# A two-layer decoder on one core: three experts of the third batch moved to the end, a two-expert distance in the last batch, and the last pair's row sums on two engines

## The chip, the core and the metric

The kernel runs on one core of one Trainium2 chip. A core has a matrix engine (TensorE, PE in the profile, with its weight loads as PEld), a vector engine (VectorE, DVE), an activation engine (ScalarE, ACT), a general engine (GpSimd, POOL) and SyncE (SP), which here only issues DMA transfers. Each engine runs its own instructions in order and waits for others by semaphores. The metric is the device time of one execution in microseconds, the median of several.

## The reference

There are four batches of 256 tokens, each token a row of 256 numbers. A batch passes through six residual steps; each normalises its input and adds its result to `x`. The last two matter here:

```python
x = x + _L1_xattn_ref(_layernorm(x), ctx_2048, ...)      # 16 query heads, 4 key heads, 1857 keys
x = x + _L1_ffn_ref(_layernorm(x), w_gate, wi_0, wi_1, wo)

# inside _L1_ffn_ref, 8 experts, 2 chosen per token
logits = jnp.dot(xf, w_gate)
top_logits, top_idx = jax.lax.top_k(logits, K)
weights = jax.nn.softmax(top_logits, axis=-1)
...
h0 = jax.lax.ragged_dot(sorted_x, wi_0, group_sizes)
h1 = jax.lax.ragged_dot(sorted_x, wi_1, group_sizes)
inter = jax.nn.silu(h0) * h1
out_sorted = jax.lax.ragged_dot(inter, wo, group_sizes)
```

The attention step is a softmax over 1857 keys for each of 16 heads; the heads are grouped by four on one key head. All of it is float32.

## The kernel before

**The step loop.** The cross attention of all four batches is one loop of steps (`steps`, L1329). A `Pair` (L1160) is two query heads of one batch and key head: 32 pairs in all, and each has eight chunks of keys (`NPAIR`), seven of 256 keys and a last one of 65. For each chunk, `score` (L1169) makes the scores `bsc` (two key blocks of 128 keys by 512 columns), copies them to `s` on ACT and keeps a running maximum `acc` on DVE. When a pair's scores are complete, `maximum` (L1188) transposes `acc` (`tm`), reduces it, and spreads it over the partitions (`bc`). Ten steps behind the scores, `exponential` (L1201) subtracts `bc` on DVE, takes the exponential on ACT and adds the chunk into `sum` on GpSimd: one addition for the first chunk (L1209), then one per key block (L1212). One step later, `weigh` (L1214) multiplies the chunk with the values into `bpo`. `finish` (L1223) copies `bpo` to `aT` on ACT, adds `sum` over the partitions with eight small matmuls (`ts`, L1232), takes the reciprocal `rs`, multiplies by the output weights (`bpw`, L1241), and adds into `x` on DVE (L1245). It is a generator in four pieces.

**Side work in the loop.** Other work is cut into generator pieces, and `put` (L1263) gives each piece a numbered place, two per step; `others` runs the pieces of a place. This is how the next key head is prepared and how the experts of batches 0, 1 and 2 are run (L1316 to L1320), 23 pieces each. The experts of batch 3 can't start before the last pair has been added into `x`, so they run alone at the very end (L1397).

**The experts.** `experts(b)` (L849) has seven pieces for normalisation, transposes (`tp`), features `yTm`, gate scores `pl`, the choice of two experts and their weights `gts`. After that there are two pieces per expert: one makes `mph` (four products, which the profile counts as eight matmuls), its `it` by a tanh on ACT and two operations on DVE (L919 to L921); the other makes `mpe` (two products, four matmuls) and adds it, weighted, into `x` with two DVE operations (L927). All eight experts are computed for every token, with weight zero for those not chosen. Weights `wi` (two transfers) and `we` (one) are loaded by SP for two experts at a time, into the `db` buffers (three of them, L162) and the `a3` buffers (three, L154). `it`, the normalised rows `mxh` and `yTm` share three buffers of the tag `a2`. PSUM products take turns over six banks (`p1`, L131).

**What sets the order.** The order of instructions on each engine is fixed when the program is built. The builder follows the written order, but if an instruction isn't ready by the builder's own estimate of times, a later one on that engine that is ready goes ahead of it. On the chip, each engine then keeps this order.

Of the kernel before, what the change touches and what calls it, by code (L numbers as in the profile page):

```python
# [15 lines left out]
AF = mybir.ActivationFunctionType  # L16
# [17 lines left out]
NROPE = 3  # L34
TERN = 20
SIDE = 24
SIDEN = 4
RATE = 1
START = (0, 3, 9, 15)
# [70 lines left out]
def decoder_kernel(ctx: ExitStack, tc: tile.TileContext, at, t, out):  # L110
# [43 lines left out]
    def fa(b, name, dt=F32):  # L154

        return fr.tile([P, 512], dt, tag=f"a{b}", name=name, bufs=NA)
# [686 lines left out]
        yield  # L843


    def ea(name):
        return fa(2, name)

    def experts(b):  # L849
        xb = xs[b]  # L850
        wgt = sm([P, 2, NE], "wgt", f"wgt{b}", 1)
        nc.sync.dma_start(out=wgt, in_=t["wgt"].rearrange("(c p) n -> p c n", p=P))
        s8 = [P, 2, NE]
        iota = cc("iota8")[:, None, :].to_broadcast(s8)
        mv = moments(xb, f"mo{b}")
        yield
        r1 = rsqrt(mv[:, :, 1], 1e-5, f"mo{b}")
        yield
        xh = centred(ea(f"mxh{b}"), xb, mv, r1)
        yield  # L860
        tp = to_features(xh, f"mo{b}")
        yT = ea(f"yTm{b}")
        A.copy(yT, tp)
        yT = yT.rearrange("p (c t) -> p c t", c=2)
        yield
        pl = p1(f"pl{b}")
        for j in range(2):
            for c in range(2):
                T.matmul(pl[:, j * 8 : j * 8 + 8], lhsT=yT[:, c, j * P : (j + 1) * P], rhs=wgt[:, c, :], start=c == 0, stop=c == 1)
        lg = sm(s8, "lg", f"mlg{b}", 1)  # L870
        V.tensor_copy(lg.rearrange("p j e -> p (j e)"), pl[:, 0:16])
        yield

        tops, hots = [], []
        for k in range(2):
            m = sm([P, 2], f"m{k}", f"mm{b}{k}", 1)
            V.tensor_reduce(m, lg, AX.X, ALU.max)
            oh = sm(s8, f"oh{k}", f"oh{b}{k}", 1)
            V.tensor_tensor(oh, lg, m[:, :, None].to_broadcast(s8), ALU.is_equal)
            V.tensor_mul(oh, oh, iota)  # L880
            ix = sm([P, 2], "ix", f"ix{b}{k}", 1)
            V.tensor_reduce(ix, oh, AX.X, ALU.min)
            V.tensor_tensor(oh, iota, ix[:, :, None].to_broadcast(s8), ALU.is_equal)
            if k == 0:
                V.scalar_tensor_tensor(lg, oh, NEG, lg, ALU.mult, ALU.add)
            tops.append(m)
            hots.append(oh)
        w2 = sm([P, 2], "w2", f"w2{b}", 1)
        V.tensor_sub(w2, tops[1], tops[0])
        A.activation(w2, w2, AF.Exp)  # L890
        yield
        w1 = sm([P, 2], "w1", f"w1{b}", 1)
        V.tensor_scalar(w1, w2, 1.0, None, ALU.add)
        V.reciprocal(w1, w1)
        V.tensor_scalar(w1, w1, 0.5, None, ALU.mult)
        V.tensor_mul(w2, w2, w1)
        gts = sm(s8, "gts", f"gts{b}", 1)
        V.tensor_mul(gts, hots[0], w1[:, :, None].to_broadcast(s8))
        V.tensor_mul(hots[1], hots[1], w2[:, :, None].to_broadcast(s8))
        V.tensor_add(gts, gts, hots[1])  # L900
        yield
        for e2 in range(0, NE, 2):
            wi = db(f"wi{b}{e2}").rearrange("p (i c n) -> p i c n", i=2, c=2)
            for i, name in enumerate(("wi0", "wi1")):
                nc.sync.dma_start(
                    out=wi[:, i], in_=t[name][:, e2 * ME : (e2 + 2) * ME].rearrange("(c p) n -> p c n", p=P)
                )
            we = weight(fa(3, f"we{b}{e2}"), "woe", e2 * ME, (e2 + 2) * ME, 0, D)
            for f in range(2):
                e = e2 + f  # L910
                ph = p1(f"mph{b}{e}")
                for i in range(2):
                    for c in range(2):
                        T.matmul(  # L914
                            ph[:, i * 256 : i * 256 + 256], lhsT=wi[:, i, c, f * ME : (f + 1) * ME], rhs=yT[:, c, :],
                            start=c == 0, stop=c == 1,
                        )
                it = ea(f"it{b}{e}")[:, 0:256]
                A.activation(it, ph[:, 0:256], AF.Tanh, scale=0.5)  # L919
                V.scalar_tensor_tensor(it, it, 1.0, ph[:, 0:256], ALU.add, ALU.mult)  # L920
                V.tensor_mul(it, it, ph[:, 256:512])  # L921
                yield
                pe = p1(f"mpe{b}{e}")
                for j in range(2):
                    T.matmul(pe[:, j * 256 : j * 256 + 256], lhsT=it[:, j * P : (j + 1) * P], rhs=we[:, f, :], start=True, stop=True)  # L925
                for j in range(2):
                    V.scalar_tensor_tensor(  # L927
                        xb[:, j, :], pe[:, j * 256 : j * 256 + 256], gts[:, j, e : e + 1], xb[:, j, :], ALU.mult, ALU.add
                    )
                yield  # L930
        nc.sync.dma_start(out=out[b].rearrange("(j p) d -> p j d", p=P), in_=xb)
        yield

    def before(b):
# [225 lines left out]
    class Pair:  # L1160


        def __init__(self, b, g, h):
# [2 lines left out]
            self.rows = [P] * (NPAIR - 1) + [LAST]  # L1166
            self.wide = [2] * (NPAIR - 1) + [1]

        def score(self, c):  # L1169

            e = gt[self.b, self.g]
            q = e["qT"][:, self.h : self.h + 2, :].rearrange("p h t -> p (h t)")
            n, w = self.rows[c], self.wide[c]
            s = s_tile(f"s{self.nm}{c}")
            self.s.append(s)
            if c == 0:
                self.acc = fa(0, f"acc{self.nm}")
            for i in range(w):
                k = 2 * c + i
                pc = p1(f"bsc{self.nm}{k}")  # L1180
                T.matmul(pc[0:n, :], lhsT=e["kT"][:, k * P : k * P + n], rhs=q, start=True, stop=True)  # L1181
                A.activation(s[0:n, i, :], pc[0:n, :], AF.Copy, scale=e["kn"][0:n, k : k + 1])  # L1182
                if k == 0:
                    V.tensor_scalar(self.acc, pc, e["kn"][:, 0:1], None, ALU.mult)  # L1184
                else:
                    V.scalar_tensor_tensor(self.acc[0:n, :], pc[0:n, :], e["kn"][0:n, k : k + 1], self.acc[0:n, :], ALU.mult, ALU.max)  # L1186
# [14 lines left out]
        def exponential(self, c):  # L1201
            n, w, s = self.rows[c], self.wide[c], self.s[c]
            V.tensor_tensor(  # L1203
                s[0:n, 0:w, :], s[0:n, 0:w, :], self.bc[0:n, None, :].to_broadcast([n, w, 512]), ALU.subtract
            )
            A.activation(s[0:n, 0:w, :], s[0:n, 0:w, :], AF.Exp)  # L1206
            if c == 0:
                self.sum = fr.tile([P, 512], F32, tag="sum", name=f"sum{self.nm}", bufs=2)
                G.tensor_tensor(self.sum, s[:, 0, :], s[:, 1, :], ALU.add)  # L1209
            else:  # L1210
                for i in range(w):
                    G.tensor_tensor(self.sum[0:n, :], self.sum[0:n, :], s[0:n, i, :], ALU.add)  # L1212
# [10 lines left out]
        def finish(self):  # L1223
# [4 lines left out]
            yield  # L1228

            ts = p1(f"ts{nm}")  # L1230
            for i in range(4):
                T.matmul(ts[:, i : i + 1], lhsT=su[:, i * P : (i + 1) * P], rhs=cc("ones")[:, 0:1], start=True, stop=True)  # L1232
            rs = sm([P, 4], "rs", f"rs{nm}")
            V.reciprocal(rs, ts[:, 0:4])
            yield

            for h in range(2):
                pw = p1(f"bpw{nm}{h}")
                for j in range(2):
                    o = h * 256 + j * P  # L1240
                    T.matmul(  # L1241
                        pw[:, j * 256 : j * 256 + 256], lhsT=aT[:, o : o + P], rhs=e["wo"][:, self.h + h, :], start=True, stop=True
                    )
                for j in range(2):
                    V.scalar_tensor_tensor(  # L1245
                        xs[b][:, j, :], pw[:, j * 256 : j * 256 + 256], rs[:, 2 * h + j : 2 * h + j + 1], xs[b][:, j, :], ALU.mult, ALU.add
                    )
                yield


    heads = [(b, g) for b in range(B) for g in range(NKV)]
# [31 lines left out]
    for n, pair in enumerate(pairs):  # L1283
# [4 lines left out]
        e += DW  # L1288
        gen = pair.finish()
        put(2 * e + 1, gen)  # L1290
        put(2 * e + 4, gen, bank=True)
        put(2 * e + 7, gen, bank=True)
        put(2 * e + 10, gen, True, bank=True)
    for k, (b, g) in enumerate(heads):
        base = 32 * (k - 1)
        if k:
# [19 lines left out]
    for b in range(B - 1):  # L1316
        gen = experts(b)
        spot = 2 * (64 * (b + 1) + 17)
        for i in range(23):
            spot = put(spot, gen, i == 22, i not in (0, 1, 2, 5, 6)) + (5 if i > 6 else 3)  # L1320

    def others(place):
        for gen, last in places.pop(place, ()):
# [70 lines left out]
    run(first)  # L1394
    run(work)
    assert not places, sorted(places)
    run(experts(B - 1))  # L1397


# [63 lines left out]
```

## Time and profile before

| | us |
|---|---|
| median of 3 runs (1830.79 to 1831.85) | 1831.21 |
| the profiled execution | 1831.5 |
| its span, first to last instruction | 1829.5 |
| TensorE busy | 1727.7 (94%) |
| DVE busy | 1300.5 (71%) |
| ACT busy | 1008.2 (55%) |
| POOL busy | 872.4 (48%) |
| mean granted TensorE clock | 0.968 |

A busy share is the time in which an engine had an instruction running, over the whole span. TensorE's share is high, but it is a mean over stages that have different limits. The page's slices of the span say more: TensorE is at nine tenths or more from the tenth slice to the 39th, and at seven in the last. The chain that ended last, followed back from the last instruction, is 70% TensorE, 10% DVE, 8% ACT, 7% POOL and 4% "issue", time in which an engine waited for nothing that the profile shows. Timeline rows give start, length, engine, line, operation, the tiles written and read, and in brackets the idle time before it and who ended that.

### The profile page before, as it was taken

How to read it: one execution, taken by the hardware profiler on the slowest of the kernel's cores; microseconds unless marked ns; L12 is line 12 of the kernel's file. 1: busy time of each engine (PE TensorE's matmuls, PEld its weight loads, DVE VectorE, ACT ScalarE, POOL GpSimd, SP SyncE). 2: the span in 40 equal slices, each digit the busy share in tenths (PEclk: the TensorE clock that was granted, in tenths of full speed). 3: DMA queues.
4: the chain of work that ended last, by engine and by line, in shares of the span. 5: the costliest groups of instructions: out<-in, count | busy, mean ns of one | idle time of the engine just before them, and what ended most of it. 6: DMA issues, size and time to landing. Idle time of an engine off the chain costs nothing.

```text
span 1829.5 us, 20298 instructions
## 1 busy us (share of the span) xinstructions
PE 1727.7 (94%) x6576; PEld 1054.0 (58%) x6576; DVE 1300.5 (71%) x2444; ACT 1008.2 (55%) x1896; POOL 872.4 (48%) x716
## 2 busy tenths in 40 slices
PE   3779899989999999999999999999999999999997
PEld 2456686655555555555555555656565655556555
DVE  6785647786777678777767786767768676766764
ACT  1556636463666565665656565565656465555541
POOL 2100232111266566656657475555656565655470
PEclk8689999989999999999999999999999999999998
DMA  4001241100210101102020211111120211011001
GB/s 140 1 22 34 71 120 62 32 24 12 81 55 9 58 26 41 38 29 66 13 67 27 64 32 52 53 38 43 41 67 29 72 32 58 21 41 49 30 29 35
DMA packets 66217, 83.01 MB, mean 45 GB/s; under 512 B 6460, under 2 KB 49600, under 8 KB 66112
## 3 DMA queue, kind: packets, MB, share of 16 engines
q1 hardware_dynamic: 64960, 80.31, 14.4%
q10 hardware_dynamic: 1152, 1.41, 0.2%
q8 instruction: 53, 0.87, 0.2%
q14 instruction: 52, 0.43, 0.1%
HBM read 80.65 MB, written 1.05 MB: 45 GB/s over the span
## 4 chain that ended last, share of the span: by engine, by line
PE 70%; DVE 10%; ACT 8%; POOL 7%; issue 4%; DMA 0%; POOLq 0%; ACTq 0%; DVEq 0%
PE bsc L1181 17%; PE bpo L1221 17%; PE pk L1115 11%; POOL sum L1212 4%; PE mph L914 2%; PE bpw L1241 2%; ACT s L1206 2%; PE xsc L562 2%; ACT s L1182 2%; PE xpo L607 2%; PE pq L1078 1%; PE mpe L925 1%; ACT sm L463 1%; POOL ropeq L1040 1%; ACT ropeq L1047 1%
## 5 line engine op out<-in xcount | busy, mean ns | idle before, releaser
L1212 POOL TENSOR_TENSOR sum<-sum,s 128x512 f32<-128x512 f32 (+1 forms) x416 | 541.0, 1300 | 82.1 <-ACT s L1206 55.8
L1181 PE MATMUL bsc<-qTb,kTb 128*128 128x512 f32 (+1 forms) x960 | 457.9, 597 | 2.7 <-ACT kTb L1126 2.7
L1221 PE MATMUL bpo<-s,vb 128*128 128x512 f32 (+1 forms) x960 | 459.1, 596 | 0.0
L1182 ACT ACTIVATE s<-bsc,kn 128x512 f32<-128x512 f32 (+1 forms) x480 | 317.7, 684 | 219.9 <-PE bsc L1181 209.4
L1186 DVE SCALAR_TENSOR_TENSOR acc<-bsc,kn,acc 128x512 f32<-128x512 f32 x448 | 333.9, 745 | 120.9 <-ACT s L1182 107.6
L1203 DVE TENSOR_TENSOR s<-s,bc 128x1024 f32<-128x1024 f32 (+1 forms) x256 | 289.4, 1143 | 16.8 <-PE bc L1199 16.7
L1206 ACT ACTIVATE s<-s 128x1024 f32<-128x1024 f32 (+1 forms) x256 | 255.8, 1005 | 47.8 <-DVE s L1203 46.1
L1181 PEld LDWEIGHTS bsc<-qTb,kTb 128*128 128x128 f32 (+1 forms) x960 | 173.5, 187 | 185.7 <-issue 141.7
L1221 PEld LDWEIGHTS bpo<-s,vb 128*128 128x128 f32 (+1 forms) x960 | 173.5, 191 | 132.7 <-issue 127.5
L1040 POOL TENSOR_TENSOR ropek<-ropek,ropuk 128x512 f32<-128x512 f32 (+1 forms) x64 | 78.2, 1222 | 242.3 <-DVE ropuk L1035 242.3
L1115 PE MATMUL pk<-wkv,cTk 128*128 128x256 f32 x832 | 190.1, 379 | 0.0
L1115 PEld LDWEIGHTS pk<-wkv,cTk 128*128 128x128 f32 x832 | 156.8, 190 | 28.3 <-issue 6.9
L1209 POOL TENSOR_TENSOR sum<-s 128x512 f32<-128x512 f32 x32 | 41.6, 1301 | 196.8 <-ACT s L1206 196.8
L1047 ACT ACTIVATE ropeq<-ropeq,rnq 128x128 f32<-128x128 f32 x128 | 41.5, 390 | 115.0 <-POOL rnq L1043 115.0
L1034 DVE TENSOR_TENSOR ropek<-pk,ctabk 128x256 f32<-128x256 f32 (+1 forms) x128 | 51.6, 403 | 55.6 <-ACT squares L1033 55.1
L1033 ACT ACTIVATE squares<-pk 128x256 f32<-128x256 f32 (+1 forms) x128 | 47.5, 373 | 64.7 <-PE pk L1115 41.6
L1118 ACT COPY vb<-pk 128x256 f32<-128x256 f32 (+1 forms) x128 | 46.0, 359 | 51.3 <-DVE ropuk L1035 48.5
L1184 DVE TENSOR_SCALAR acc<-bsc,kn 128x512 f32<-128x512 f32 x32 | 24.0, 749 | 62.8 <-ACT s L1182 62.8
L1241 PEld LDWEIGHTS bpw<-wo,aT 128*128 128x128 f32 x256 | 48.7, 191 | 34.2 <-issue 27.0
L463 ACT ACTIVATE sm<-sc,mx 128x128 f32<-128x128 f32 (+1 forms) x128 | 52.2, 436 | 27.3 <-DVE mx L456 20.2
L1241 PE MATMUL bpw<-wo,aT 128*128 128x256 f32 x256 | 66.3, 382 | 0.0
L1043 POOL TENSOR_TENSOR kn<-ssk,nhalf 128x4 f32<-128x4 f32 (+1 forms) x64 | 66.0, 1032 | 0.0
(487 smaller groups left out, 2483.8 us busy)
## 6 DMA issues: line engine op xcount, KB each, us to landing
cTk<-in_ctxT SPq DMA_DIRECT2D x32, 512.0 KB, 3.7
wq<-in_wq SPq DMA_DIRECT2D x16, 512.0 KB, 5.2
wo<-in_wo SPq DMA_DIRECT2D x16, 512.0 KB, 3.9
wi<-in_wi SPq DMA_DIRECT2D x32, 256.0 KB, 2.9
xcT<-in_ctxT SPq DMA_DIRECT2D x12, 512.0 KB, 3.7
xct<-in_ctx SPq DMA_DIRECT2D x12, 512.0 KB, 3.7
cTk<-in_ctxT SPq DMA_DIRECT2D x16, 384.0 KB, 3.2
wkv<-in_wkv SPq DMA_DIRECT2D x16, 256.0 KB, 3.8
```

The costliest lines, as they stand in the source:

```text
L463: A.activation(ex[:, h, k], scs[u][:, h, k], AF.Exp, bias=mx[:, j, i : i + 1], accum_out=sums[:, j, i : i + 1])
L1040: G.tensor_tensor(r4, r4, u4[:, :, ::-1, :], ALU.add)
L1043: G.tensor_tensor(rn, ss[:, 0:n], nhalf[:, 0:n], ALU.pow)
L1115: T.matmul(pk[:, q, :], lhsT=src, rhs=e["wkv"][:, c, :], start=c == 0, stop=c == 1)
L1181: T.matmul(pc[0:n, :], lhsT=e["kT"][:, k * P : k * P + n], rhs=q, start=True, stop=True)
L1182: A.activation(s[0:n, i, :], pc[0:n, :], AF.Copy, scale=e["kn"][0:n, k : k + 1])
L1186: V.scalar_tensor_tensor(self.acc[0:n, :], pc[0:n, :], e["kn"][0:n, k : k + 1], self.acc[0:n, :], ALU.mult, ALU.max)
L1203: V.tensor_tensor(s[0:n, 0:w, :], s[0:n, 0:w, :], self.bc[0:n, None, :].to_broadcast([n, w, 512]), ALU.subtract)
L1206: A.activation(s[0:n, 0:w, :], s[0:n, 0:w, :], AF.Exp)
L1212: G.tensor_tensor(self.sum[0:n, :], self.sum[0:n, :], s[0:n, i, :], ALU.add)
L1221: T.matmul(self.po, lhsT=e["v"][0:n, k, :], rhs=self.s[c][0:n, i, :], start=k == 0, stop=k == NCH - 1)
L1241: T.matmul(pw[:, j * 256 : j * 256 + 256], lhsT=aT[:, o : o + P], rhs=e["wo"][:, self.h + h, :], start=True, stop=True)
```

## The change

It has three parts.

- The loop runs 17 instead of 23 pieces of batch 2's experts, so experts 5, 6 and 7 (`KEPT = 3`) are left. They run after the loop, in turn with the first three pieces (moments, reciprocal root, normalised rows) of batch 3's experts. After them comes the rest of batch 3's.
- In the last batch, `outer(e - 2)` is written after `inner(e)`, so the second product of an expert stands two experts behind the first. Its `it` takes buffers of the tag `a1`, its `mxh` and `yTm` of `a0`; `gts` has a tile of its own. Each batch's result is stored in two halves, the last batch's second half by ACT's queue.
- In the last pair, the last three chunks are added up on DVE in a tile `rest` (four additions), the first five on GpSimd as before (nine additions). `ts` adds both tiles, with twice as many matmuls. The pair's `finish` is one piece after `aT` instead of three.

```diff
+KEPT = 3
 def experts(b):
+        final = b == B - 1
+        def ea(name, place=0):
+            return fa(place if final else 2, name)
...
-        gts = sm(s8, "gts", f"gts{b}", 1)
+        gts = sm(s8, f"gts{final}", f"gts{b}", 1)
...
+        def inner(e):
+            e2 = e - e % 2
+            if e == e2:
+                wi = db(f"wi{b}{e2}").rearrange("p (i c n) -> p i c n", i=2, c=2)
...
+                weights[e2] = wi, weight(fa(3, f"we{b}{e2}"), "woe", e2 * ME, (e2 + 2) * ME, 0, D)
...
+            it = ea(f"it{b}{e}", 1)[:, 0:256]
+            A.activation(it, ph[:, 0:256], AF.Tanh, scale=0.5)
+            V.scalar_tensor_tensor(it, it, 1.0, ph[:, 0:256], ALU.add, ALU.mult)
+            V.tensor_mul(it, it, ph[:, 256:512])
+            return it
+
+        def outer(e, it):
+            pe = p1(f"mpe{b}{e}")
...
+        ahead = 2 if final else 0
+        its = []
+        for e in range(NE + ahead):
+            if e < NE:
+                its.append(inner(e))
+                if not final:
+                    yield
+            if e >= ahead:
+                outer(e - ahead, its[e - ahead])
+            yield
+        for j in range(2):
+            (nc.scalar if final and j else nc.sync).dma_start(out=out[b, j * P : (j + 1) * P], in_=xb[:, j, :])
...
 class Pair:
+            self.final = (b, g, h) == (B - 1, NKV - 1, 2)
+            self.own = NPAIR - 3 if self.final else NPAIR
...
+            elif c == self.own:
+                self.rest = fa(0, f"rest{self.nm}")
+                V.tensor_add(self.rest, s[:, 0, :], s[:, 1, :])
+            elif c > self.own:
+                for i in range(w):
+                    V.tensor_add(self.rest[0:n, :], self.rest[0:n, :], s[0:n, i, :])
...
+            parts = (su, self.rest) if self.final else (su,)
             for i in range(4):
-                T.matmul(ts[:, i : i + 1], lhsT=su[:, i * P : (i + 1) * P], rhs=cc("ones")[:, 0:1], start=True, stop=True)
+                for a in parts:
+                    T.matmul(
+                        ts[:, i : i + 1], lhsT=a[:, i * P : (i + 1) * P], rhs=cc("ones")[:, 0:1],
+                        start=a is parts[0], stop=a is parts[-1],
+                    )
...
+        pieces = 23 if b < B - 2 else 23 - 2 * KEPT
+        for i in range(pieces):
             spot = put(spot, gen, i == 22, i not in (0, 1, 2, 5, 6)) + (5 if i > 6 else 3)
+    kept = gen
...
-    run(experts(B - 1))
+    gen = experts(B - 1)
+    for _ in range(KEPT):
+        next(gen)
+        next(kept)
+        next(kept)
+    run(kept)
+    run(gen)
```

More of the change, by code (lines that the diff above doesn't have):

```diff
@@ L843, in recurrence @@
         yield
-    def ea(name):
-        return fa(2, name)
     def experts(b):
         xb = xs[b]
+        final = b == B - 1
+        def ea(name, place=0):
+            return fa(place if final else 2, name)
         wgt = sm([P, 2, NE], "wgt", f"wgt{b}", 1)
@@ L901, in experts @@
         yield
[L902 to L906, printed above, removed]
-                )
[L908 to L930, printed above, removed]
@@ L931, in experts @@
-        nc.sync.dma_start(out=out[b].rearrange("(j p) d -> p j d", p=P), in_=xb)
+        weights = {}
+        def inner(e):
+            e2 = e - e % 2
+            if e == e2:
+                wi = db(f"wi{b}{e2}").rearrange("p (i c n) -> p i c n", i=2, c=2)
+                for i, name in enumerate(("wi0", "wi1")):
+                    nc.sync.dma_start(
+                        out=wi[:, i], in_=t[name][:, e2 * ME : (e2 + 2) * ME].rearrange("(c p) n -> p c n", p=P)
+                    )
+                weights[e2] = wi, weight(fa(3, f"we{b}{e2}"), "woe", e2 * ME, (e2 + 2) * ME, 0, D)
+            wi = weights[e2][0]
+            ph = p1(f"mph{b}{e}")
+            for i in range(2):
+                for c in range(2):
+                    T.matmul(
+                        ph[:, i * 256 : i * 256 + 256], lhsT=wi[:, i, c, e % 2 * ME : (e % 2 + 1) * ME], rhs=yT[:, c, :],
+                        start=c == 0, stop=c == 1,
+                    )
+            it = ea(f"it{b}{e}", 1)[:, 0:256]
[3 more added lines that the diff above has]
+            return it
@@ new lines, in outer @@
+        def outer(e, it):
+            pe = p1(f"mpe{b}{e}")
+            for j in range(2):
+                T.matmul(
+                    pe[:, j * 256 : j * 256 + 256], lhsT=it[:, j * P : (j + 1) * P], rhs=weights[e - e % 2][1][:, e % 2, :],
+                    start=True, stop=True,
+                )
+            for j in range(2):
+                V.scalar_tensor_tensor(
+                    xb[:, j, :], pe[:, j * 256 : j * 256 + 256], gts[:, j, e : e + 1], xb[:, j, :], ALU.mult, ALU.add
+                )
@@ L932, in experts @@
+        ahead = 2 if final else 0
[8 more added lines that the diff above has]
+            yield
+        for j in range(2):
+            (nc.scalar if final and j else nc.sync).dma_start(out=out[b, j * P : (j + 1) * P], in_=xb[:, j, :])
         yield
@@ L1230, in finish @@
             ts = p1(f"ts{nm}")
+            parts = (su, self.rest) if self.final else (su,)
             for i in range(4):
-                T.matmul(ts[:, i : i + 1], lhsT=su[:, i * P : (i + 1) * P], rhs=cc("ones")[:, 0:1], start=True, stop=True)
+                for a in parts:
+                    T.matmul(
+                        ts[:, i : i + 1], lhsT=a[:, i * P : (i + 1) * P], rhs=cc("ones")[:, 0:1],
+                        start=a is parts[0], stop=a is parts[-1],
+                    )
             rs = sm([P, 4], "rs", f"rs{nm}")
             V.reciprocal(rs, ts[:, 0:4])
-            yield
+            if not self.final:
+                yield
             for h in range(2):
@@ L1247, in finish @@
                     )
-                yield
+                if not self.final:
+                    yield
     heads = [(b, g) for b in range(B) for g in range(NKV)]
@@ L1290, in decoder_kernel @@
         put(2 * e + 1, gen)
-        put(2 * e + 4, gen, bank=True)
-        put(2 * e + 7, gen, bank=True)
-        put(2 * e + 10, gen, True, bank=True)
+        if not pair.final:
+            put(2 * e + 4, gen, bank=True)
+        put(2 * e + 7, gen, pair.final, bank=True)
+        if not pair.final:
+            put(2 * e + 10, gen, True, bank=True)
     for k, (b, g) in enumerate(heads):
@@ L1318, in decoder_kernel @@
         spot = 2 * (64 * (b + 1) + 17)
-        for i in range(23):
+        pieces = 23 if b < B - 2 else 23 - 2 * KEPT
+        for i in range(pieces):
             spot = put(spot, gen, i == 22, i not in (0, 1, 2, 5, 6)) + (5 if i > 6 else 3)
+    kept = gen
     def others(place):
```

## The prediction

> **What bounds the kernel now.** I read the page first, then the stretch table of the last 95 us (its columns: stretch, length, then busy time of PE, PEld, DVE, ACT, POOL, granted TensorE clock, DMA share, GB/s), then the chain of waits and the timeline there.
>
> ```profile
> 1735.00:1785.40 50.40, 50.40 (x165) 28.49 (x163) 34.03 (x50) 24.08 (x32) 34.15 (x27) 1.00 0.11 33
> 1785.40:1787.10 1.70, 0.10 (x2) 0.01 (x1) 0.00 (x0) 0.59 (x1) 1.56 (x2) 1.00 0.29 100
> 1787.10:1790.65 3.55, 3.51 (x16) 2.57 (x16) 1.06 (x3) 0.00 (x0) 0.00 (x0) 0.80 0.00 0
> 1790.65:1798.20 7.55, 3.23 (x13) 2.54 (x13) 2.08 (x8) 1.68 (x3) 0.71 (x1) 0.50 0.00 0
> 1798.20:1804.20 6.00, 6.00 (x19) 4.87 (x19) 3.56 (x22) 0.59 (x2) 0.00 (x0) 0.61 0.00 0
> 1809.00:1825.50 16.50, 14.58 (x64) 11.88 (x64) 8.40 (x20) 1.93 (x5) 0.00 (x0) 1.00 0.01 2
> ```
>
> Up to 1785.40 TensorE is busy all the time at full clock: work taken out there shortens the time one for one. After that the last pair and the last batch's experts stand alone. TensorE has holes, and from 1790.65 to 1798.20 it gets half its clock.
>
> ```profile
> 1739.85 1.73 PE mph L914 x8
> ...
> 1753.63 0.86 PE mpe L925 x4
> ...
> 1785.78 1.26 POOL sum L1212
> 1787.04 5.61 issue
> ...
> 1798.22 5.92 PE mph L914 x16
> ...
> 1810.12 3.45 PE mph L914 x16
> ```
>
> The chain shows what one expert takes of a full TensorE: 1.73 + 0.86 = 2.59 us. It also shows GpSimd's last sum at the hand-over, and the same 16 matmuls at 5.92 us cold and 3.45 us warm.
>
> ```profile
> 1768.21 1.30 POOL L1209 TENSOR_TENSOR sum<-s 128x512 f32<-128x512 f32 x1 [10.36 <-ACT s L1206]
> 1769.59 17.46 POOL L1212 TENSOR_TENSOR sum<-sum,s 128x512 f32<-128x512 f32 x13
> ...
> 1785.54 0.59 ACT L1227 COPY aT<-bpo 128x512 f32<-128x512 f32 x1 [7.61 <-PE bpo L1221]
> 1787.10 1.05 PE L1232 MATMUL ts<-cst,sum 128*128 128x1 f32 x8 [1.60 <-POOL sum L1212]
> 1788.01 2.60 PE L1241 MATMUL bpw<-wo,aT 128*128 128x256 f32 x8
> ```
>
> From the timeline: the last pair's output is finished at 1785.54 (where its copy aT starts), but the row sums `ts` wait for GpSimd until 1787.10.
>
> ```profile
> 1366.43 1.00 POOL L1040 TENSOR_TENSOR ropek<-ropek,ropuk 128x384 f32<-128x384 f32 x1 [9.96 <-DVE ropuk L1035]
> 1366.67 1.78 DVE L1004 TENSOR_TENSOR ctabk<-ang,knw 128x960 f32<-128x960 f32 x1
> 1367.39 1.78 POOL L1043 TENSOR_TENSOR kn<-ssk,nhalf 128x3 f32<-128x3 f32 x1
> ```
>
> This L1004 begins 0.24 us into a GpSimd operation and takes 1.78 us; with GpSimd idle, near 293 us, it takes 1.15. The GpSimd power behind it, usually 1.01, also takes 1.78. They hold each other up.
>
> [...]
>
> **The change part by part**, against the profiled execution (1831.5 us: span 1829.5 and 2.0 around it).
>
> 1. *Experts 5, 6, 7 of the third batch leave the loop.* All their TensorE work (first product at 1739.85, 1761.8 and 1774.2, second at 1753.6, 1766.4 and 1781.9) lies in the full stretch: 3 x 2.59 = 7.77 us. Their ACT (0.38) and DVE work (2 x 0.42 + 2 x 0.44 = 1.7 each) leaves too, none of it limiting. What could be late next is the exponentials: in the last pair the first is done 2.45 us after `bc` (1765.69 to 1768.14), then DVE subtracts a chunk every 1.2 us while TensorE uses one every 1.72, so they stay ahead. aT starts at 1785.54 - 7.77 = 1777.8. **-7.8.**
>
> 2. *Sums shared.* GpSimd made 14 sums in 1787.04 - 1768.21 = 18.83 us, 1.345 each. It keeps 1 + 4 x 2 = 9. `bc` comes earlier by expert 5 and the first product of expert 6, 2.59 + 1.73 = 4.3 us, so sums start at 1763.9 and would end at 1776.0, before aT. Alone, the old 14 would have ended at 1782.7: without this part most of step 1 would be lost at `ts`. DVE adds 1 + 2 + 1 = 4 sums of 0.68 us with two SBUF inputs, while GpSimd still has three or four to do. [...] My walk: sixth exponential done at 1771.7, then adds and GpSimd's sums alternate, and the last add ends near 1779.0, 1.2 us after aT's start. The `ts` matmuls double to 16, 2 x 0.79 = 1.6 us instead of 0.9. aT to bpw becomes 1.2 + 1.6 - 0.2 (they may start a bit before aT) = 2.6, against 2.47 now. Bounds: -1.1 without lock, +1.5 if it costs twice that. **+0.1.**
>
> 3. *bpw warm.* TensorE no longer rests before it: 8 matmuls take 2 x 0.86 = 1.72 instead of 2.60. **-0.9.** The pieces of the finish are merged into one; all of the old ones stood alone here already, so that costs nothing. [...]
>
> 4. *From bpw's end to the last mpe's end,* now 1790.61 to 1825.55 = 34.9 us. New: kept experts 7.77 (their inputs are ready; they fill the wait for normalisation, 3.0 us from bpw's end to the first mxh and 1.1 more); transposes tp 0.44; copy yT 0.59 with its hand-overs, 0.85; pl 0.86 when warm (as the eight ts matmuls); eight experts at 2.59 = 20.7. Two experts of distance cover the 1.4 us from mph's end to mpe (1817.04 to 1818.41), so the holes in 1807.60 to 1809 and after go. DVE has 1.7 of every 2.59 us, ACT 0.4; the top-two chain (some 20 instructions of 0.17 to 0.2 us, about 5 us) lies beside three first products, 5.2 us. I add 0.8 for waits I cannot place, such as kept expert 7's second product. Sum 31.4 + 0.15 hand-over = 31.6. Bounds: 29.9 (copy hidden, no waits) to 35 (rival A). **-3.3.**
>
> 5. *Output in halves.* The first half leaves after its own addition; the second goes by ACT's queue, idle then. The store of 256 KB takes 2.1 us to landing and 0.38 to issue. I take **-0.2**, bounds 0 and -0.5.
>
> 6. *DMA and buffers.* SP gets one more store per earlier batch, 0.38 us of issue, hidden by TensorE. Kept weights hold buffers of `db` and `a3` longer: the last batch's second pair of weights can load only when kept expert 5's first product is done (about 1783), is there after 0.88 + 2.9 = 3.8 us, and is needed about 1795. The third waits for kept expert 7, needed 11 us later; the fourth for expert 1, four experts (10 us) ahead. On SP the third batch's store waits for the last kept addition, about 1790, and loads behind it still have 5 us. Cost 0; uncovered it is rival C. The separate gates tile and `it` in the aT slots add no wait, their last readers being done.
>
> Sum: -7.8 + 0.1 - 0.9 - 3.3 - 0.2 = -12.1, so 1831.5 - 12.1 = 1819.4. The three timed runs have a median 0.3 below the profiled one, so I say **1819.0**.
>
> **Rivals.**
> A. *The kept experts are a serial block.* Written ahead of the last batch's transposes, each waits its 1.4 us (3 x 1.4 = 4.2) and the DVE and ACT queues hold the normalisation behind their products. In place of 0.8 us of waits, 4.2: 1822.5. For: the order on each engine is fixed by the build's own estimate of times; DVE and ACT run in order. Against: the build already moved second products behind later first ones in the last batch (mph x16).
> B. *The kept work is pulled back into the loop.* In the trace ts and bpw of the pair before stand ahead of their written places, in front of the first bpo. If the kept matmuls fill such places, aT stays at 1785.5 and the end stays cold: without GpSimd's wait -1.1, with two experts of distance in the last batch 27.3 us (1798.2 to 1825.5) becomes 20.7 + 2.5 cold = 23.2, so -4.1, store -0.2: 1826. Against: elsewhere the loop keeps the written order, since TensorE has no hole.
> C. *Slower: weight loads become exposed* in the last batch, by a store or kept load ahead on SP's queue. A pair that is asked for only when needed costs 3.8 us, and 2.5 more for the cold clock behind such a hole (5.92 - 3.45): 6.3. Two pairs, 12.6, use up the gain and decide the sign; three give 1819 + 19 = 1838. Against it are the leads of step 6.
> D. *Even better:* no lock, waits filled, copy hidden: -1.2 - 0.8 - 0.85, 1816.
> E. *The tail absorbs all:* within 0.2%.
>
> **How the numbers follow.** My case 0.60 (its own range 1817 to 1821.5), A 0.12, B 0.10, C 0.07, D 0.08, E 0.03. A, B, D and my case are faster by over 0.2%: 0.90; E 0.03; C 0.07. 0.2% is 3.7 us, about what a measurement of this kernel can tell from no change. The range 1814.5 to 1823.5 holds D, mine and A, 0.8.
>
> **What would show it.** Step 1: aT of the last pair near 1778, no mph of the third batch between the last pair's bpo. Step 2: the last adds on DVE longer than 0.68 us, GpSimd's late sums longer than 1.3, ts starting within 2 us of aT. Step 3: bpw 1.7 to 1.9 us. Step 4: granted clock near 1 from the pair's end on, and six kept product groups between bpw and tp; mph of the last batch 2.59 us apart per expert without idle TensorE. Step 6: wi landing at least 4 us before its mph. Idle TensorE on weights, or aT near 1785, would make it wrong.

## The result, and the profile after

The changed kernel takes **1817.59 us** (median of 5 runs, 1812.34 to 1818.97), the kernel before 1831.21 (5 runs, 1830.79 to 1831.85). The ratio is 0.9922, 95% interval 0.9909 to 0.9935: 13.6 us less. 1819.0 was forecast.

The profiled execution happens to be the shortest one, 1812.34 us with a span of 1810.6. So the two spans must not be subtracted as they are. Up to the step loop the order of instructions is the same in both kernels, yet the loop's first `tm` stands at 499.9 us in the trace before and at 493.2 in the trace after. So that 6.7 us is not work that the change took out; the last section shows what differs there. I measure everything below from the first `tm` (the mark) of each trace. In what follows TensorE is *warm* at the full granted clock (1.00 in the tables) and *cold* at half of it (0.50), a *hole* is a time in which it has nothing to run, and the *hand-over* is the passage from the loop's last pair to the last batch's experts.

| us from the mark | before | after | difference |
|---|---|---|---|
| last `bc` ends | 1265.8 | 1261.5 | -4.3 |
| last `aT` starts | 1285.6 | 1277.9 | -7.7 |
| last sum ends (GpSimd / DVE) | 1287.1 / none | 1277.1 / 1277.6 | |
| last pair's `ts` starts | 1287.2 | 1277.7 | -9.5 |
| last pair's `bpw` | 1288.1 to 1290.7 | 1280.4 to 1282.2 | -8.5 at its end |
| last batch's first `mph` | 1298.2 | 1292.5 | -5.7 |
| last `mpe` ends | 1325.6 | 1313.4 | -12.2 |
| end of the span | 1329.6 | 1317.3 | **-12.3** |

From the mark to the end the change takes 12.3 us off; the forecast sum was -12.1. The other 1.3 us of the 13.6 between the medians probably lie ahead of the mark; the timed runs other than the profiled ones left no trace that could show it. The table of stretches of the changed kernel, with the same columns as in the prediction:

```profile
1720.00:1770.90 50.90, 50.90 (x153) 26.07 (x152) 38.97 (x50) 25.79 (x33) 30.35 (x23) 1.00 0.00 0
1770.90:1775.30 4.40, 4.40 (x30) 4.07 (x29) 0.85 (x3) 0.59 (x1) 0.00 (x0) 1.00 0.00 0
1775.30:1783.00 7.70, 6.09 (x29) 5.02 (x28) 4.57 (x16) 2.24 (x5) 0.71 (x1) 1.00 0.31 102
1783.00:1806.60 23.60, 23.52 (x114) 20.30 (x112) 16.62 (x56) 3.86 (x10) 0.00 (x0) 1.00 0.25 79
```

TensorE is now full through the hand-over and the last batch, with one hole of 1.6 us between 1775.30 and 1783.00, and the clock stays at 1.00. Before, the wait for normalisation ran at 0.50. The timeline of the changed kernel shows the hand-over itself:

```profile
1771.12 0.59 ACT L1260 COPY aT<-bpo 128x512 f32<-128x512 f32 x1 [5.33 <-PE bpo L1254]
...
1772.62 1.11 PE L921 MATMUL mph<-yTm,wi 128*128 128x256 f32 x4
...
1773.57 1.89 PE L1280 MATMUL bpw<-wo,aT 128*128 128x256 f32 x8
...
1777.93 1.13 PE L934 MATMUL mpe<-we,it 128*128 128x256 f32 x4 [1.61 <-DVE it L928]
...
1785.67 5.43 PE L921 MATMUL mph<-yTm,wi 128*128 128x256 f32 x24
```

`bpw` is warm at 1.89 us (2.60 before). Half of kept expert 5's first product stands ahead of it. The one hole of 1.61 us is the wait for that expert's `it`. The last batch then begins with three first products in a row, 24 matmuls in 5.43 us; 16 of them took 5.92 before. The chain of the changed kernel (start, length, what) shows the new end:

```profile
1796.28 0.86 PE mpe L934 x4
1797.14 1.73 PE mph L921 x8
1798.87 0.86 PE mpe L934 x4
1799.73 1.73 PE mph L921 x8
...
1806.87 0.47 DVE x L939
1807.34 0.39 DVEq L1510
```

The products follow each other without a gap, 2.59 us per expert, and no wait for ACT or DVE stands between them until the last one.

### The profile page after: what moved, and what is told of

Its sections match the earlier page's. It is cut to its first block, busy times and chain, and to the rows that moved or that the text cites. A ratio compares the mean times of both kernels' runs of the same rounds, so it can differ in the third digit from the quotient of the medians.

```text
span 1810.6 us, 20324 instructions
## 1 busy us (share of the span) xinstructions
PE 1717.0 (95%) x6584; PEld 1049.5 (58%) x6584; DVE 1305.6 (72%) x2448; ACT 1008.2 (56%) x1896; POOL 867.0 (48%) x711
## 4 chain that ended last, share of the span: by engine, by line
PE 73%; DVE 10%; ACT 8%; POOL 6%; issue 3%; DMA 0%; ACTq 0%; POOLq 0%; DVEq 0%
PE bpo L1254 18%; PE bsc L1208 18%; PE pk L1139 11%; POOL sum L1245 3%; PE bpw L1280 3%; PE mph L921 2%; ACT s L1233 2%; PE xsc L563 2%; ACT s L1209 2%; PE xpo L608 2%; PE pq L1102 2%; PE mpe L934 1%; ACT sm L464 1%; POOL ropeq L1064 1%; PE tpk L1148 1%
## 5 line engine op out<-in xcount | busy, mean ns | idle before, releaser
L1245 POOL TENSOR_TENSOR sum<-sum,s 128x512 f32<-128x512 f32 (+1 forms) x411 | 535.5, 1303 | 81.7 <-ACT s L1233 55.9
```

## The experiments

All are cut from the changed kernel. "From the mark" is the time from the first `tm` to the end of the span in each run's trace: 1317.3 for the changed kernel, 1329.6 for the one before. The traces differ before the mark, though every engine has the same order of instructions there, so these numbers tell more than the medians where a microsecond or two matter. Each is of one execution. Up to the last `aT` they repeat well: it starts 1277.8 or 1277.9 us from the mark in the five kernels with three experts kept behind `ts`, and 1285.6 in the three that keep none. The merged finish, the tile changes and the halved store stand in every run below, so none of them was priced on its own by a removal. The medians of the kernel before beside these runs were 1830.06 to 1830.65 us.

### All sums on GpSimd

```diff
-            self.own = NPAIR - 3 if self.final else NPAIR
+            self.own = NPAIR
-            parts = (su, self.rest) if self.final else (su,)
+            parts = (su,)
```

> The changed kernel, but all 14 sums of the last pair stay on GpSimd. Theory 1 (the sums set the hand-over once the three experts are gone): GpSimd's sums take 14 x 1.345 = 18.8 us from the first exponential, which was done at bc + 2.5 us, so they end at bc + 21.3, while aT starts at bc + 16.4 in the trace of the changed kernel. ts waits about 5 us behind aT's start, TensorE [...]is cold for the next products: 5 to 7 us slower than the changed kernel, 6.5 to 8.5 us faster than before. Rival (the kept experts fill the wait, so sharing is worth nothing): within 1 us of the changed kernel.

1824.69 us, ratio to before 0.9968 (0.9957 to 0.998); from the mark 1324.6, **7.3 us more** than the changed kernel. The timeline and the stretches of this run:

```profile
1776.71 0.58 ACT L1260 COPY aT<-bpo 128x512 f32<-128x512 f32 x1 [5.81 <-PE bpo L1254]
1781.66 1.87 PE L1267 MATMUL ts<-cst,sum 128*128 128x1 f32 x8 [4.99 <-POOL sum L1245]
1783.39 2.05 PE L921 MATMUL mph<-yTm,wi 128*128 128x256 f32 x4
1785.24 3.15 PE L1280 MATMUL bpw<-wo,aT 128*128 128x256 f32 x8
```

```profile
1776.00:1782.00 6.00, 1.01 (x4) 0.34 (x2) 0.00 (x0) 0.58 (x1) 5.29 (x5) 0.91 0.00 0
1782.00:1786.00 4.00, 4.00 (x14) 3.55 (x14) 0.18 (x1) 0.00 (x0) 0.00 (x0) 0.50 0.00 0
```

TensorE waits 4.99 us for the last sum, and then runs at half clock: `ts` takes 1.87 us (eight matmuls; 0.95 warm), half an `mph` 2.05 (1.11) and `bpw` 3.15 (1.89), 3.1 us more together. Wait and cold clock, less the eight matmuls saved in `ts`, make the 7.3. The kept experts could have filled that wait, but they stand behind `ts` in TensorE's order, so the rival falls. The sums do set the hand-over once the experts are gone. The price lies a little outside the range: 7.3 us where 5 to 7 was expected, and 5.0 faster than before (from the mark) where it was 6.5 to 8.5.

### No distance in the last batch

```diff
-        ahead = 2 if final else 0
+        ahead = 0
```

> The changed kernel, but each second product of the last batch is written right behind its first one. Theory 1 (the distance hides the 1.4 us from mph to mpe): the last batch takes what the kernel before takes warm, 27.3 less 2.5 = 24.8 us from its first mph to its last mpe, against 21 with the distance: 3.5 to 4.5 us slower than the changed kernel. Rival (the build reorders the products anyway, so the distance is worth little): under 1.5 us slower.

1820.7 us, ratio 0.9944 (0.9927 to 0.996); from the mark 1321.3, **4.0 us more**. In the timeline of this run the holes are back:

```profile
1801.05 1.10 PE L934 MATMUL mpe<-we,it 128*128 128x256 f32 x4 [1.49 <-issue]
...
1810.44 1.13 PE L934 MATMUL mpe<-we,it 128*128 128x256 f32 x4 [1.39 <-DVE it L928]
...
1816.41 1.13 PE L934 MATMUL mpe<-we,it 128*128 128x256 f32 x4 [0.52 <-DVE it L928]
```

The first hole, put down to "issue", ends 0.1 us after DVE has finished that expert's `it` (1800.94). The build does reorder some products, so not every expert waits. The three holes shown make 1.49 + 1.39 + 0.52 = 3.4 us of the 4.0; the last batch takes 25.1 us from its first `mph` to its last `mpe`, 21.0 with the distance. That is as theory 1 had it, and the rival falls.

### No expert kept

```diff
-KEPT = 3
+KEPT = 0
```

> The changed kernel with no expert kept: all 23 pieces of the third batch run in the loop; sums shared and distance stay. Theory 1 (the kept work fills the rest of TensorE at the hand-over and keeps its clock up): aT comes 7.8 us later, the wait for normalisation stands empty again, its clock at half, and the time is 5.5 to 7 us longer than that of the changed kernel, about 7 us shorter than before. Rival (TensorE's work only moves, and what leaves the loop comes back at the end): within 1.5 us of the changed kernel, so that the gain came from the other two parts.

1824.24 us, ratio 0.9965 (0.9952 to 0.9978); from the mark 1324.4, **7.1 us more**. `aT` starts at 1285.6 from the mark, as in the kernel before. The stretches of this run show the empty wait and the cold experts behind it:

```profile
1787.50:1795.00 7.50, 3.23 (x13) 2.54 (x13) 2.03 (x8) 1.68 (x3) 0.71 (x1) 0.71 0.00 0
1795.00:1801.00 6.00, 6.00 (x16) 4.77 (x16) 3.57 (x22) 0.59 (x2) 0.00 (x0) 0.51 0.00 1
```

So the kept work fills time that was empty; it is not merely moved. The run is 5.2 us faster than the kernel before (from the mark), where about 7 was expected.

### Two and four experts kept

```diff
-KEPT = 3
+KEPT = 2   (the other run: 4)
```

> The changed kernel with two experts kept instead of three. Theory 1 (the hole holds about two experts; in the trace of the changed kernel mxh is ready 3.1 us before tp starts, so the third only delays it): aT 2.6 us later, tp as much earlier behind bpw, the same time within 1 us. Rival (every kept expert is worth its 2.6 us): 2 to 3 us slower than the changed kernel.

> The changed kernel with four experts kept. Theory 1 (TensorE is full on both sides of the move): aT 2.6 us earlier, the end as much later: the same time as with three within 1 us, up to 1.8 us more if bpw runs at half clock, as it did in the run with two kept, whose bpw also stands right behind the many one-column matmuls of ts. Rival (each further expert pays): 2 to 3 us faster than the changed kernel.

Two: 1817.19 us, ratio 0.9927 (0.9912 to 0.9942), from the mark 1317.7, 0.4 more than with three. Four: 1815.59 us, ratio 0.9918 (0.9904 to 0.9931), from the mark 1316.4, 0.9 less. Both are within what theory 1 gives, and neither is told apart from the changed kernel by its interval. The run with two lost time that the trace shows:

```profile
1774.00:1777.40 3.40, 3.40 (x9) 1.51 (x8) 3.24 (x3) 0.00 (x0) 2.75 (x2) 1.00 0.00 0
1777.40:1779.10 1.70, 1.70 (x17) 1.67 (x15) 0.00 (x0) 0.58 (x1) 0.00 (x0) 1.00 0.00 0
1779.10:1782.60 3.50, 3.50 (x10) 2.81 (x10) 1.06 (x3) 0.00 (x0) 0.00 (x0) 0.52 0.00 0
```

Its timeline has the cold `bpw` and the wait for the first kept expert's `it`; the last line is `bpw` in the run with four:

```profile
1779.13 3.66 PE L1280 MATMUL bpw<-wo,aT 128*128 128x256 f32 x8
...
1786.61 1.13 PE L934 MATMUL mpe<-we,it 128*128 128x256 f32 x4 [0.36 <-DVE it L928]
...
1774.16 1.97 PE L1280 MATMUL bpw<-wo,aT 128*128 128x256 f32 x8
```

`bpw` got half its clock (0.52) although TensorE is shown busy all the time before it: the stretch ahead holds the 16 one-column matmuls of `ts`. In the run with four kept the same order gave a warm `bpw` of 1.97 us. So this is not certain to happen; here it cost 1.7 us (3.66 and 1.97). That two are as good as three therefore has two parts: the cold `bpw` takes 1.7 us, and the hole before the first kept second product is 0.36 us in place of 1.61. Beyond two, further experts brought nothing that these runs can tell from zero. Keeping one was not run.

### The first kept product ahead of `ts`

This takes the hole of 1.61 us out.

```diff
     kept = gen
+    put(2 * (NPAIR * len(pairs) - 1 + DW) + 6, kept)
...
-    for _ in range(KEPT):
+    for i in range(KEPT):
         next(gen)
         next(kept)
-        next(kept)
+        if i < KEPT - 1:
+            next(kept)
```

> The changed kernel, but the first product of kept expert 5 is written ahead of the last pair's ts, so that its second product is ready behind bpw. In the trace of the changed kernel TensorE rests 1.6 us there (from 1776.3 to 1777.9). Theory 1 (the end is bound by TensorE, so a hole taken out shortens it): 1 to 2 us faster than the changed kernel. Rival (the chain of the normalisation sets the end, mxh to tp to yT): no difference, within 0.5 us.

1817.3 us, ratio 0.992 (0.9907 to 0.9932); from the mark 1315.9, **1.4 us less**. `mpe` of kept expert 5 now follows `bpw` without a wait, in the timeline of this run:

```profile
1774.24 1.97 PE L1280 MATMUL bpw<-wo,aT 128*128 128x256 f32 x8
1776.05 1.03 PE L934 MATMUL mpe<-we,it 128*128 128x256 f32 x4
1776.91 3.62 PE L921 MATMUL mph<-yTm,wi 128*128 128x256 f32 x16
```

The trace bears out theory 1. A smaller hole is left, 0.68 us for the last batch's `yTm`. The edit also let the build pull half of this first product further up, behind the `ts` of the pair before, as rival B of the prediction had it for the kept work. The medians (1817.3 against 1817.59) can't show 1.4 us, because they scatter by several microseconds, probably for the reason given at the end. I don't claim it as a faster kernel.

### The same with four and with two kept

> Four experts kept, with the first kept product ahead of the last pair's ts as in the run with the first product early. If TensorE's holes are what is left at the end, this closes them all (about 0.9 us were left in that run, at mxh and yT): 0 to 1 us less than that run from the first tm to the end, 1.5 to 2.5 us less than the changed kernel. If the work only moves, it equals that run.

> Two experts kept, with the first kept product ahead of the last pair's ts. TensorE then has to wait for kept expert 7's second product (1.4 us) and for yT (0.8 us) with nothing to put there: about 1 to 1.5 us more from the first tm to the end than with three kept in that form. If two fill the hole, the same within 0.5 us.

Four: 1817.43 us, ratio 0.9931 (0.9918 to 0.9943), from the mark 1317.1. This is 1.2 more than with three, where 0 to 1 less was expected: a miss. A hole of 1.48 us came up before kept expert 5's second product, since the build put nothing between that expert's first and second product:

```profile
1783.87 1.10 PE L934 MATMUL mpe<-we,it 128*128 128x256 f32 x4 [1.48 <-DVE it L928]
```

Two: 1818.42 us, ratio 0.9934 (0.9921 to 0.9948), from the mark 1317.7, 1.8 more than with three, somewhat more than the 1 to 1.5 expected. Its two holes are the ones named, 1.38 us for `it` and 0.68 for `yTm`. No version ran that clearly beats the changed kernel.

### The kept experts alone, and the sums alone

The kept experts alone are the first two edits above together. The sums alone are `KEPT = 0` with `ahead = 0`.

> The kernel before with the three kept experts alone: no sums on DVE, no distance. Theory 1 (the parts need each other: without the other two the kept experts move TensorE's work behind GpSimd's wait): the losses of the two single removals add up, 7.3 + 4.0 of 12.3 us, which leaves 0 to 2.5 us faster than before. Rival (each part has a worth of its own, that of the kept experts 7 us): 6 to 8 us faster than before.

> The kernel before with the shared sums alone: none kept, no distance. Theory 1: GpSimd's last sum ends 1.5 us behind aT's start there, so little is to be had: ts starts at once, bpw 1 us earlier and warm (0.7): 1.2 to 2.2 us faster than before. Rival (sharing is worth the 7.3 us that its removal cost): 6 us or more faster than before.

Kept alone: 1829.85 us, ratio 0.9994 (0.9986 to 1.0002), from the mark 1328.7. That is 0.9 less than before, and no difference by the interval. Sums alone: 1827.9 us, ratio 0.9985 (0.9979 to 0.9992), from the mark 1326.9: 2.7 less. The first was foretold by adding the two single losses (12.3 - 7.3 - 4.0 = 1.0). The second gave 0.5 more than its range: besides the 1.7 us up to the last batch's first `mph`, its last batch takes 26.6 us and not 27.4. The timeline of the run with the kept experts alone shows what ate their gain:

```profile
1782.04 1.87 PE L1267 MATMUL ts<-cst,sum 128*128 128x1 f32 x8 [5.00 <-POOL sum L1245]
1783.77 2.05 PE L921 MATMUL mph<-yTm,wi 128*128 128x256 f32 x4
1785.62 3.20 PE L1280 MATMUL bpw<-wo,aT 128*128 128x256 f32 x8
```

`aT` is there 7.7 us earlier, but TensorE then waits 5.00 us for GpSimd and runs `ts`, `mph` and `bpw` cold. What left the loop comes back as this wait and this slowness. The same three experts are worth 7.1 us in the changed kernel and 0.9 alone. The runs also say which partner they need. With the sums shared but no distance they are worth 5.6 us (1326.9 without them, 1321.3 with them), so most of the difference comes from the sums. The distance is worth 2.5 us beside the sums alone (1326.9 to 1324.4), 4.1 beside the kept experts alone (1328.7 to 1324.6) and 4.0 beside both; the distance alone was not run.

### Two chunks on DVE instead of three

```diff
-            self.own = NPAIR - 3 if self.final else NPAIR
+            self.own = NPAIR - 2 if self.final else NPAIR
```

> The changed kernel with DVE adding only the last two chunks (two additions), GpSimd the first six (11). GpSimd starts 2.4 us behind bc; 11 sums at 1.36 us and two delays of 0.32 us by DVE's additions end at bc + 18.0, where aT starts at bc + 16.4: ts 1.5 us later, TensorE idle so long but not cold: 1 to 2 us slower than the changed kernel. If the mutual blocking with DVE's additions is what costs (three delayed sums and three additions of 1.6 instead of 0.7 us there), fewer additions make it no slower.

1821.45 us, ratio 0.9955 (0.9939 to 0.997); from the mark 1320.9, 3.6 us more. The wait was as expected, and its price was higher, as the timeline of this run shows:

```profile
1776.44 0.38 PE L1267 MATMUL ts<-cst,sum 128*128 128x1 f32 x2 [1.65 <-POOL sum L1245]
...
1779.33 3.45 PE L1280 MATMUL bpw<-wo,aT 128*128 128x256 f32 x8
```

`bpw` takes 3.45 us, 1.5 more than warm: behind 1.65 us of idle time, 1.8 us of one-column matmuls and half an `mph` the clock fell (0.72 granted from 1779 to 1785 us, where the 5 us before had 1.00). I had said "not cold", so that half of the expectation is wrong. Three chunks is better than two and than none; four were not tried. With three, the last addition ends 0.3 us before `aT` starts.

## Why the prediction was right

**Step 1, experts out of the loop: -7.8 forecast, -7.7 measured** (start of `aT`). `bc` came 4.3 us earlier, as worked out. The exponentials stayed ahead of TensorE.

**Step 2, shared sums: +0.1 forecast, 0.0 measured for `aT` to `bpw`** (2.48 and 2.45 us). The net is right by luck, since its terms are not. The prediction's lock is DVE and GpSimd slowing each other, as at its L1004 (1.78 us each in place of 1.15 and 1.01). I priced it at 1.2 us behind `aT`, an estimate that put 0.68 us for one addition on DVE (line L820 of the kernel before, 128x512, takes 0.67 to 0.69) beside some 1.3 us for one of GpSimd's sums; the last addition ended 0.3 us before `aT` started. In its place half of a kept first product, 0.95 us, stands between `ts` and `bpw`. That the two slow each other is there, in the timeline of the changed kernel:

```profile
1758.56 11.73 POOL L1245 TENSOR_TENSOR sum<-sum,s 128x512 f32<-128x512 f32 x8
...
1763.69 0.77 DVE L1239 TENSOR_TENSOR rest<-s 128x512 f32<-128x512 f32 x1
...
1765.90 4.93 DVE L1242 TENSOR_TENSOR rest<-rest,s 128x512 f32<-128x512 f32 x3
```

The three later additions take 1.57 to 1.64 us each, where the first takes 0.77. All four end 0.54 to 0.56 us after the GpSimd sum beside them has ended, so an addition is long when it starts early in such a sum (0.2 to 0.6 us into it for the three, 1.06 for the first). Three of GpSimd's eight sums here take 1.6 us where the others take 1.26 to 1.29. My walk started the sixth chunk's addition at 1771.7, 10.3 us behind `bc`; it started 9.0 us behind. And three additions held up GpSimd by 0.3 us each and not by 0.68, the fourth by nothing. GpSimd loses only about half an addition (0.3 of 0.68 us). When each of its three late sums starts, an addition is already under way and has 0.46 to 0.48 us left to run.

**Step 3, `bpw` warm: -0.9 forecast, -0.7 measured** (2.60 to 1.89). In most of the runs the clock was full (1.00) where TensorE had work, and 0.50 or 0.51 behind a rest: 4.99 us ahead of `ts` with all sums on GpSimd, 3.66 us ahead of `tp` with none kept. The run with two kept is the exception, at 0.52 without any rest. The runs give no length of rest that decides it: 1.65 us of waiting went before a cold `bpw` in the run with two chunks on DVE (0.72 in that stretch), and 1.60 us before one that is cold in part in the kernel before (0.80).

**Step 4, from `bpw`'s end to the last `mpe`: -3.3 forecast, -3.7 measured** (34.9 to 31.2 us). The total is near, but the terms differ. Half a kept first product (0.95 us) had been done ahead of `bpw`, so less was left. The copy `yTm`, priced at 0.85, lies beside kept expert 7's second product, which runs behind `tp`. Against these, the waits came to 1.6 us in one hole, not 0.8. In the last batch, distance and warm clock worked as described: 21.0 us from the first `mph` to the last `mpe`, where 20.7 was worked out and the kernel before takes 27.4.

**Step 5, halves of the output: -0.2 forecast, -0.1 measured** (last `mpe`'s end to the span's end, 4.03 and 3.92 us).

**Step 6, DMA: nothing, as forecast.** The second, third and fourth pairs of weights were asked for at 1776.35, 1782.54 and 1789.40 us. Their first products came 10 to 13 us later (1789.1, 1794.39 and 1799.57).

The rivals: A (waits of a serial block) shows in its first part, 1.6 of the 4.2 us; B (kept work pulled back into the loop) hardly occurred, half a product ahead of `bpw` being all of it; C, the slower side, had no trace of exposed weights; of D (better still) two of three parts came true, no cost of the lock behind `aT` and a hidden copy, while the waits were not filled; E, no change, is ruled out by the interval. So the path and the large terms were right, the smaller errors cancelled, and part of the agreement in the medians is chance, since the stretch ahead of the mark alone moves by up to 6.8 us between traces.

## What to carry to other kernels

Work that is ready at any time is worth most where an engine must wait for a serial chain: take it out of a stretch in which that engine is full, and give it as much as the empty stretch holds, where two did as well as three or four. Before moving it, ask what will be late at the hand-over once the full stretch is shorter. Here it was GpSimd's sums: the kept experts were worth 0.9 us with neither of the other edits, 5.6 with the sums shared, 7.1 with both. Price such parts together: their single removals cost 7.3, 4.0 and 7.1 us, 18.4 in all, out of 12.3.

## What was not expected of the hardware

**Ahead of the loop the same instructions take different times.** The mark stands at 499.9 us in the trace before, 493.2 in the one after, and between 493.3 and 500.0 in the experiments. In the stretch from 50 to 100 us the granted clock was 0.74 or 0.75 in the six traces whose mark is at 499.0 or later, and 0.83 to 0.85 in the seven whose mark is earlier. From 380 to 420 us it was 0.96 in the two earliest (493.2 and 493.3) and 0.84 to 0.92 in all others. The clock records of the whole stretch up to the mark tell it more plainly: the time at half clock adds up to 71.7 us in the trace after and to 92.2 in the trace before. The timed runs of the changed kernel lie up to 6.6 us apart, probably for this reason: the mean granted clock of the shortest is 0.978, that of the other four 0.973 or 0.974. Clock records by stretch are of the profiled executions alone. What sets it in a given execution stays open.

**Half clock comes in pieces of 3.41 us.** From 300 us on to the end of the last `mph`, every stretch of half clock in the traces before and after lasts 3.41 us or a multiple of it (3.41, 6.83 or 13.65). Behind the last pair it is 13.65 us in the kernel before and none in the changed kernel. The granted clocks in the stretches of other runs come near the same lengths: 10.2 us at half clock with none kept, 6.8 with all sums on GpSimd, 3.4 with two kept and with two chunks on DVE. The cold `bpw` of the run with two kept lies in such a piece, and its price of 1.7 us is half of it.

**A busy TensorE can still lose its clock.** Sixteen one-column matmuls, 1.7 us without a gap, were followed by a half-clock `bpw` in the run with two kept (3.66 us), and by a warm one (1.97 us) in the runs with four kept, with none and with the sums alone. With 1.65 us of idle time ahead of them it was cold too (3.45 us, two chunks on DVE). In the two runs with the first product early and three or four kept, where a kept first product, or half of it, stands right ahead of `ts`, `bpw` was warm (1.97 us); whether its place guards the clock was not tested further.
